# A graph's edges counted in BF16, with a bound in place of a look at the counts, in a graph network kernel on one Trainium2 core

## The chip, the core and the metric

The kernel runs on one core of a Trainium2 chip. A core has a matrix engine (PE; its weight loads are shown as PEld), a vector engine (DVE), a scalar engine (ACT), a general engine (POOL), a queue for transfers (SP) and DMA engines that move data between the chip's memory and the core. Each engine works through its own list of instructions in order; semaphores tie the lists together. The metric is the time of one execution on the device, in microseconds; lower is better.

## The reference

A graph network over N = 3125 nodes with D = 256 features. There are two edge lists: list a, 100000 edges (src, dst) sorted by dst, and list b, 65536 edges of a graph attention layer (GAT). Cut to what matters here:

```python
xn = layernorm(x)
x = x + gnn0(xn) + mix(xn)          # convolution over list a; 4 layers of linear attention and feed-forward
x = x + ffn0(layernorm(x))          # GAT over list b gates four experts
xn = layernorm(x)
x = x + gnn1(xn) + attention1(xn)   # two aggregations over list a; linear attention
x = x + ffn1(layernorm(x))          # eight experts, the two best for each row

def gnn0(x):
    agg = segment_sum(x[src], dst, num_segments=N)
    return batchnorm((x + agg) @ W.T + b)

# in GAT, with a loop added for every node
e = leaky_relu(a_src[src] + a_dst[dst], negative_slope=0.2)
ee = exp(e - segment_max(e, dst)[dst])
alpha = ee / (segment_sum(ee, dst)[dst] + 1e-16)
agg = segment_sum(h[src] * alpha, dst)
```

Every segment sum over a list is computed as a product with a matrix of counts: entry (s, d) says how often the edge from s to d is in the list.

## The kernel before

**Counting.** The matrix AT (FP32, 3125 x 3125, in the chip's memory) holds the counts of list a, C those of list b. Both are first cleared by 25 transfers of 1528 KB each (`clear`, L454). Then each list is taken in columns of 128 edges; a's has 782 columns, b's 512. `Edges.prepare` (L311) finds for every edge how many equal ones come before it in a window of columns: one DVE comparison a column (L343, in `prepare_tail` L383) with its output in a scratch tile `junk`, whose sum goes to `val`, and five small operations a chunk (L353 to L357) that make the addresses. `scatter` (L390) then adds `val` to the matrix with one indirect transfer a column, issued by POOL (L394). Scatters of one window are free of each other; a window waits for the window before.

**The order of the edge work.** The generator `both` (L413) writes it out: eight chunks of list a are prepared before the mix starts, then chunks of a alone, then pairs of a window of a (5 or 4 columns) with two columns of b; last comes the rest of b, 198 columns in windows of 16. The mix calls `beside` after each of its steps, which moves the generator on by 1.05 steps. Scatters of both lists stand on POOL in that order. Between two barriers (`tc.no_sync_barrier`) a list scheduler of the framework may exchange instructions on an engine; POOL's order of the lists is held by explicit dependencies.

**The mix.** Four layers, each with a QKV part (L564 to L578), a softmax part (to L617) and an output and feed-forward part whose results are added to xs on DVE (L639, L652).

**The convolution.** After the barrier at L695, `aggregate` (L657) reads AT row block by row block (`ch`, L673), takes the greatest count of each block on DVE (L675, into `most`), and multiplies the FP32 rows of `xn` with it (L680); L688 adds the node itself with an identity. `done0` (L709) copies the sums to aT, multiplies with the weights and collects batch norm's statistics.

**GAT.** The front (L821) normalises xs and makes the attention terms; the first pass (L872 on) reads C as `cnt` (L880), turns it into penalties on ACT (L884) and takes maxima on DVE (L887, output in a scratch tile `am` with one buffer). The second pass (L917 on) weighs and sums. In it `copy_counts` has POOL copy AT to A1, the same counts in BF16, in 25 pieces (L933), and `most` becomes `more`, which says whether a count is over 256, so that BF16 doesn't hold it exactly.

**Layer 1.** `sums` (L1406) multiplies three BF16 parts of each row (`parts`) with A1 (L1430). A branch (`if_more`, L1595 and L1651) adds what A1 lost; with these inputs `more` is 0 and the branch is passed over.

Of the kernel before, what the change touches and what calls it, by code (L numbers as in the profile page):

```python
# [17 lines left out]
P = 128  # L18
# [27 lines left out]
COLS = 32  # L46
CLR = 3056
# [37 lines left out]
def tile_gps(ctx: ExitStack, tc: tile.TileContext, a, out):  # L85
# [207 lines left out]
    class Edges:  # L293
# [7 lines left out]
        def __init__(self, ep, w_before, dump, key, width, used, rows, mat, tag):  # L301
            self.ep, self.w_before, self.dump = ep, w_before, dump
            self.key, self.used, self.rows = key, used, rows
            self.flat = mat.rearrange("(n o) -> n o", o=1)
            self.val = ep.tile([P, width], F32, name=f"val{tag}", tag=f"val{tag}")
            self.idx = key[:, :].bitcast(I32)
            self.before, self.started, self.queued = [], [], []
            self.width, self.made, self.have = width, 0, (0, 0)
            self.ps = None

        def prepare(self, cols, win):  # L311
# [7 lines left out]
            for c in range(c0, c1, win):  # L319
# [20 lines left out]
                for j in range(k):  # L340
                    junk = ep.tile([P, WIDE * P], BF16, name="junk", tag="junk", bufs=2)
# [12 lines left out]
            V.scalar_tensor_tensor(sel[:, :w], val, BEFORE, sel[:, :w], op0=OP.is_lt, op1=OP.mult)  # L354
            V.tensor_tensor(rel[:, :w], kc, dump[:, :w], op=OP.subtract)
# [4 lines left out]
        def prepare_tail(self, c, k):  # L360
# [9 lines left out]
            for j in range(k):  # L370
                for i, (h, w) in enumerate(halves):
                    junk = ep.tile([P, WIDE * P], BF16, name="junk", tag="junk", bufs=2)
# [17 lines left out]
        def scatter(self, c, end, other=None):  # L390

            if c < self.used:
# [3 lines left out]
                    in_=self.val[:, c:c + 1], in_offset=None, compute_op=OP.add)  # L396
# [16 lines left out]
    def both(ea, eb, clear_b):  # L413
# [27 lines left out]
        while eb.made < eb.width:  # L441
            c0 = eb.made
            yield from eb.prepare(COLS, TAIL)
            for c in range(c0, eb.made):
                eb.scatter(c, (c - c0) % TAIL == TAIL - 1 or c == eb.made - 1)
# [4 lines left out]
    with ExitStack() as st:  # L450
# [3 lines left out]
        def clear(mat):  # L454

            m = mat.rearrange("(p b f) -> p b f", p=P, f=CLR // 4)
            for b in range(25):
                nc.sync.dma_start(m[:, 4 * b:4 * b + 4, :], zero[:, None, :].to_broadcast([P, 4, CLR // 4]))
                yield
# [10 lines left out]
        first, later = clear(AT), clear_own()  # L470
# [5 lines left out]
        steps(first, 4)  # L476
        with tc.tile_pool(name="ps_keys", bufs=1, space=PSUM) as ps:
            key_a = keys(ep, ps, a["src"], a["dst"], E0, True, "a")
            steps(first, 3)
# [35 lines left out]
        ea = Edges(ep, w_before, dumpf, *key_a, AT, "a")  # L515
        behind = both(ea, Edges(ep, w_before, dumpf, *key_b, C2, "b"), later)
# [140 lines left out]
    def aggregate(ps, ap, X, nfb, self_id, passes, done, most, shared):  # L657


        for groups in passes:  # L660
            c0, c1 = 512 * groups[0], min(N, 512 * (groups[-1] + 1))
            bank, acc = None, {}
            for i, g in enumerate(groups):
                if g == shared:
                    bank = ps.tile([P, nfb, P], F32, name="agb", tag="agb", bufs=1)
                for fb in range(nfb):
                    acc[fb, i] = (bank[:, fb, :] if g == shared else
                                  ps.tile([P, 512], F32, name=f"ag{fb}_{i}", tag=f"ag{fb}_{i}", bufs=1))
            for s in range(NT):
                r = rows_of(s)  # L670
                ch = ap.tile([P, 512 * 3 + cols_of(NG - 1)], F32, name="ch", tag="ch", bufs=3)
                for q0, q1 in split_rows(r):
                    nc.sync.dma_start(ch[q0:q1, :c1 - c0], AT2[s * P + q0:s * P + q1, c0:c1])  # L673
                at = passes.index(groups) * NT + s
                V.tensor_reduce(most[:r, at:at + 1], ch[:r, :c1 - c0], axis=AX.X, op=OP.max)  # L675
                for fb in range(nfb):
                    w = X[:r, s, fb * P:(fb + 1) * P]
                    for i, g in enumerate(groups):
                        n = cols_of(g)
                        T.matmul(acc[fb, i][:, :n], lhsT=w, rhs=ch[:r, i * 512:i * 512 + n],  # L680
                                 start=s == 0 and (g != shared or fb == 0),
                                 stop=s == NT - 1 and (g != shared or fb == nfb - 1), skip_group_check=g == shared)
                if s == 0:
                    for fb in range(nfb):
                        for i, g in enumerate(groups):
                            for j, t in enumerate(tiles_of(g)):
                                q = rows_of(t)
                                T.matmul(acc[fb, i][:, j * P:j * P + q], lhsT=X[:q, t, fb * P:(fb + 1) * P],  # L688
                                         rhs=self_id[:q, :q], start=False, stop=False, skip_group_check=g == shared)
            for i, g in enumerate(groups):  # L690
                for fb in range(nfb):
                    done(i, g, fb, acc[fb, i], cols_of(g))
# [3 lines left out]
    most_p = ctile([P, 1], "most_p")  # L696
    more = ctile([1, 1], "more", I32)
    with ExitStack() as st:
        gp = st.enter_context(tc.tile_pool(name="gnn0", bufs=1))
        xn = gp.tile([P, NT, D], F32, name="xn", tag="xn")  # L700
        for g in range(NG):
            load_rows(xn[:, 4 * g:4 * g + len(tiles_of(g)), :], xn_d, g)
# [4 lines left out]
        stats = gp.tile([P, 2, NG, 6], F32, name="stats", tag="stats")  # L707
        with tc.tile_pool(name="ps_g0", bufs=1, space=PSUM) as ps:
            def done0(i, g, fb, p, n):  # L709
                if fb:  # L710
                    S.activation(aT[:, fb, 512 * g:512 * g + n], p[:, :n], AF.Copy)
# [8 lines left out]
                else:  # L720
                    V.tensor_copy(aT[:, fb, 512 * g:512 * g + n], p[:, :n])

            most = gp.tile([P, 2 * NT], F32, name="most", tag="most")
            V.memset(most, 0.0)
            aggregate(ps, gp, xn, 2, ident, [[0, 1, 2], [3, 4, 5, 6]], done0, most, NG - 1)
            V.tensor_reduce(most_p, most, axis=AX.X, op=OP.max)
# [54 lines left out]
    with ExitStack() as st:  # L781
# [135 lines left out]
        with ExitStack() as st2:  # L917
# [5 lines left out]
            p = ptile()  # L923
            T.transpose(p[:1, :P], most_p, ident)
            V.tensor_reduce(most_p[0:1, :], p[0:1, :P], axis=AX.X, op=OP.max)
            V.tensor_scalar(more, most_p[0:1, :], MOST, None, op0=OP.is_gt)
            copies = iter(range(25))

            def copy_counts(after):

                b = next(copies, None) if after else None
                if b is not None:
                    d = G.dma_start(out=A1.rearrange("(p f) -> p f", p=P)[:, CLR * b:CLR * (b + 1)],  # L933
                                    in_=AT.rearrange("(p f) -> p f", p=P)[:, CLR * b:CLR * (b + 1)])
                    tc.add_manual_dep(d.ins, after.ins.name, Edges.after, reason="beside the second pass")

# [77 lines left out]
            def summed(g, s, ex, c, m, state):  # L1014
# [6 lines left out]
                for h in range(4):  # L1021
                    at = 20 * s + 5 * h
                    o = T.matmul(pa[32 * h:32 * h + 32, c:c + m], lhsT=hgp[:r, at:at + 32], rhs=ex[:r, h, c:c + m],  # L1023
                                 start=(s == 0), stop=(s == NT - 1))
                if c + m < n:
                    return
                if s % 3 == 2:
                    copy_counts(state.get("gone"))
                    state["gone"] = o
# [365 lines left out]


    def parts(pool, x, xb):

        r, w = x.shape
        rest = pool.tile([P, w], F32, name="rest", tag="rest", bufs=3)[:r]  # L1400
        S.activation(xb[:, 0, :], x, AF.Copy)
        G.tensor_tensor(rest, x, xb[:, 0, :], op=OP.subtract)
        S.activation(xb[:, 1, :], rest, AF.Copy)
        G.tensor_tensor(xb[:, 2, :], rest, xb[:, 1, :], op=OP.subtract)

    def sums(ps, ap, Xb, nfb, passes, done, shared=None):  # L1406


        for groups in passes:
            c0, c1 = 512 * groups[0], min(N, 512 * (groups[-1] + 1))  # L1410
            bank = None
            acc = {}
            for i, g in enumerate(groups):
                if g == shared:
# [383 lines left out]
```

## Time and profile before

| | us |
|---|---|
| median of 3 runs | 5104.12 |
| the three runs | 5093.92, 5104.12, 5104.90 |
| the profiled execution, whole | 5094.23 |
| its span | 5092.4 |
| PE busy in the span | 4003.0 |
| DVE busy | 3218.2 |
| POOL busy | 2769.6 |
| ACT busy | 1467.1 |

The profile records one execution; its span is the time from its first to its last record, and 1.8 us of the execution lie around it. The granted clock of PE was 0.865 of full speed over the span. A line of a group names the kernel's line, engine, operation, output and input, then count, busy time, mean duration in ns, and the idle time of the engine in front of these instructions with what ended it. A line of a timeline has the start in us from the span's start, the duration, the instruction, and in brackets the idle time before it with its releaser. The stages in the trace: the mix with the edge work from the start to about 2257, the convolution and GAT's front to 2682, GAT's first pass to 3057, its second to about 3690, then layer 1.

### The profile page before, as it was taken

How to read it: one execution, taken by the hardware profiler on the slowest of the kernel's cores; microseconds unless marked ns; L12 is line 12 of the kernel's file. 1: busy time of each engine (PE TensorE's matmuls, PEld its weight loads, DVE VectorE, ACT ScalarE, POOL GpSimd, SP SyncE). 2: the span in 40 equal slices, each digit the busy share in tenths (PEclk: the TensorE clock that was granted, in tenths of full speed). 3: DMA queues.
4: the chain of work that ended last, by engine and by line, in shares of the span. 5: the costliest groups of instructions: out<-in, count | busy, mean ns of one | idle time of the engine just before them, and what ended most of it. 6: DMA issues, size and time to landing. Idle time of an engine off the chain costs nothing. (4 is left out here: it accounts for less than half of the span.)

```text
span 5092.4 us, 48980 instructions
## 1 busy us (share of the span) xinstructions
PE 4003.0 (79%) x16189; PEld 2300.3 (45%) x16189; DVE 3218.2 (63%) x8074; ACT 1467.1 (29%) x2293; POOL 2769.6 (54%) x1860
## 2 busy tenths in 40 slices
PE   1457888878766877849979964666689998999999
PEld 1234455445544454524446641222245444544477
DVE  7978887898899874113348996889973031331231
ACT  0311133114111321200014448989740021000033
POOL 0668888888888888877760006888620031001034
PEclk6668888889787878969989986888899999999999
DMA  9954444444332322247656536543291212212266
GB/s 371 329 117 74 83 72 55 81 79 56 26 26 17 34 16 1 5 88 138 131 101 216 186 123 176 138 121 104 84 280 55 83 50 70 64 54 68 57 170 169
DMA packets 457112, 530.76 MB, mean 104 GB/s; under 512 B 213682, under 2 KB 354779, under 8 KB 451798
## 3 DMA queue, kind: packets, MB, share of 16 engines
q1 hardware_dynamic: 256058, 494.24, 30.7%
q0 software_dynamic: 200784, 33.23, 13.9%
q8 instruction: 133, 2.18, 0.2%
q14 instruction: 137, 1.11, 0.1%
HBM read 397.41 MB, written 169.95 MB: 111 GB/s over the span
## 5 line engine op out<-in xcount | busy, mean ns | idle before, releaser
L394 POOL DMA_INDIRECT AT<-vala,keya x782 | 1232.6, 1576 | 421.0 <-issue 221.0
L394 POOL DMA_INDIRECT C<-valb,keyb x512 | 807.6, 1577 | 203.4 <-issue 143.0
L988 POOL TENSOR_TENSOR ex<-ex,pqb 128x1024 f32<-128x1024 f32 (+3 forms) x200 | 367.0, 1857 | 434.0 <-ACT ex L987 433.4
L343 DVE SCALAR_TENSOR_TENSOR junk<-kr,keya,w_before 128x640 bf16<-128x640 f32 (+2 forms) x729 | 573.1, 830 | 0.6 <-DMA kr<-keys_a 0.6
L383 DVE SCALAR_TENSOR_TENSOR junk<-kr,keyb,w_before 128x1024 bf16<-128x1024 f32 (+1 forms) x390 | 482.3, 1269 | 4.5 <-DMA kr<-keys_b 4.4
L194 PE MATMUL tr<-ident,rows 128*128 128x128 f32 (+1 forms) x500 | 103.4, 361 | 465.8 <-ACT rows L180 441.0
L228 PE MATMUL mm<-hT,w 128*128 128x512 f32 (+1 forms) x896 | 418.2, 632 | 17.2 <-ACT hT L196 16.9
L1430 PE MATMUL ag<-chb,Hb 128*128 128x512 bf16 (+1 forms) x1800 | 420.1, 387 | 13.0 <-DMA chb<-A 13.0
L887 DVE CUSTOM_DVE_ANT_0 am<-asb,pen 128x1664 f32<-128x1664 f32 (+3 forms) x200 | 357.3, 1786 | 51.0 <-ACT pen L884 41.0
L649 PE MATMUL o<-w,hid 128*128 128x256 f32 (+1 forms) x1600 | 383.0, 393 | 0.0
L1023 PE MATMUL pa<-ex,hgp 128*32 128x512 f32 (+3 forms) x1400 | 208.4, 676 | 197.1 <-DVE ex L1011 193.9
L1011 DVE SCALAR_TENSOR_TENSOR ex<-ex,ct 128x2048 f32<-128x2048 f32 (+3 forms) x175 | 345.7, 2007 | 23.4 <-ACT ex L1004 13.8
L1004 ACT ACTIVATE ex<-ex,as 128x1024 f32<-128x1024 f32 (+3 forms) x400 | 345.2, 932 | 3.4 <-DVE ex L993 2.9
L649 PEld LDWEIGHTS o<-w,hid 128*128 128x128 f32 (+1 forms) x1600 | 296.9, 190 | 79.4 <-issue 34.7
L1259 POOL DMA_INDIRECT slots<-rb,r_ati x50 | 49.8, 997 | 516.2 <-DVE rb L1252 407.6
L680 PE MATMUL ag<-ch,xn 128*128 128x512 f32 (+1 forms) x600 | 272.5, 602 | 62.3 <-issue 62.3
L231 ACT ACTIVATE hid<-mm,fm 128x512 f32<-128x512 f32 (+1 forms) x336 | 211.1, 632 | 370.4 <-PE mm L228 353.0
L228 PEld LDWEIGHTS mm<-hT,w 128*128 128x128 f32 x896 | 191.7, 233 | 234.9 <-issue 190.0
L194 PEld LDWEIGHTS tr<-ident,rows 128*128 128x128 f32 (+1 forms) x500 | 66.7, 174 | 506.6 <-ACT rows L180 469.2
L180 ACT ACTIVATE rows<-xs,ln_nmr,rs_y 128x256 f32<-128x256 f32 (+1 forms) x200 | 105.7, 592 | 649.0 <-DVE ln_nmr L173 625.1
L1430 PEld LDWEIGHTS <-Hb 128*128 128x128 bf16 (+1 forms) x2100 | 184.9, 99 | 226.9 <-issue 35.1
L675 DVE TENSOR_REDUCE most<-ch 128x1 f32<-128x1536 f32 (+3 forms) x50 | 89.0, 1780 | 228.7 <-DMA ch<-AT 228.5
(430 smaller groups left out, 6962.5 us busy)
## 6 DMA issues: line engine op xcount, KB each, us to landing
AT<-zero SPq DMA_DIRECT2D x25, 1528.0 KB
C<-zero SPq DMA_DIRECT2D x25, 1528.0 KB
cnt<-C SPq DMA_DIRECT2D x24, 1562.5 KB
cd<-C SPq DMA_DIRECT2D x36, 1024.0 KB
kr<-keys_b SPq DMA_DIRECT2D x64, 512.0 KB
f1w<-in_f_w_dram SPq DMA_DIRECT2D x56, 512.0 KB
slots<-blank SPq DMA_DIRECT2D x15, 1820.0 KB
kr<-keys_a SPq DMA_DIRECT2D x48, 512.0 KB
```

The lines of the kernel that those rows point to most:

```text
L228: T.matmul(ph[:, :n], lhsT=w1[:, k, hb * P:(hb + 1) * P], rhs=xT[:, k, :n], start=(k == 0), stop=(k == 1))
L231: S.activation(h[:, :n], ph[:, :n], AF.Gelu, bias=bias[hb])
L343: V.scalar_tensor_tensor(junk[:, :k * P], self.kr[:, at:at + k * P], key[:, c + j:c + j + 1], self.w_before[:, u:u + k * P], op0=OP.is_equ ...
L383: V.scalar_tensor_tensor(out, kk, key[:, c + j:c + j + 1], by, op0=OP.is_equal, op1=OP.mult, accum_out=more[:, j:j + 1] if i else self.val ...
L394: s = G.indirect_dma_start(out=self.flat, out_offset=bass.IndirectOffsetOnAxis(ap=self.idx[:, c:c + 1], axis=0), in_=self.val[:, c:c + 1], ...
L649: T.matmul(po[:r], lhsT=hid[hb][:, j * P:j * P + r], rhs=w2[:, hb, :], start=(hb == 0), stop=False)
L680: T.matmul(acc[fb, i][:, :n], lhsT=w, rhs=ch[:r, i * 512:i * 512 + n], start=s == 0 and (g != shared or fb == 0), stop=s == NT - 1 and (g ...
L887: V.tensor_tensor_reduce(out=junk[:r, :w], in0=asb[:r, h, c0:c1], in1=pen[:r, :w], scale=1.0, scalar=-3.0e38, op0=OP.subtract, op1=OP.max, ...
L988: G.tensor_tensor(e, e, pq[:r, h, :n], op=OP.add)
L1004: S.activation(ex[:r, h, :n], ex[:r, h, :n], AF.Exp, bias=sc)
L1011: V.scalar_tensor_tensor(e4, e4, 1.0, ct[:r, None, :m].to_broadcast([r, 4, m]), op0=OP.min, op1=OP.mult)
L1430: T.matmul(acc[fb, g][:, :n], lhsT=Xb[:r, s, i, fb * P:(fb + 1) * P], rhs=ch[:r, at:at + n], start=first, stop=last, skip_group_check=g == ...
```

## The change

List a is counted straight into A1 in BF16; AT is neither cleared nor filled unless a branch asks for it. While a list with a BF16 matrix is prepared, each chunk also notes, for either half of the targets, the greatest count that a window adds at one place (`most`); the sum of these over the windows is a bound on every count in that half. `at_most` forms the two sums after the mix, and `more` says whether the larger is over 256. If it is, `recount` clears AT, scatters all of list a again in FP32, copies AT to A1, and `residue` adds what A1 lost. The convolution uses `sums` with three BF16 parts of the rows, made in front of the branch, and an identity in BF16 for the node itself. The 198 last columns of b are prepared as before, but their scatters stand behind the branch. The scratch tile `junk` has one buffer instead of two. GAT's second pass has no copies any more.

```diff
@@ class Edges, __init__
+            self.low = None
+            if mat.dtype == BF16:
+                self.low = ep.tile([P, width], BF16, name=f"low{tag}", tag=f"low{tag}")
+                self.most, self.windows = ep.tile([P, 2, MOSTW], BF16, name=f"most{tag}", tag=f"most{tag}"), 0
+                V.memset(self.most, 0.0)
@@ prepare, and the same in prepare_tail
-                    junk = ep.tile([P, WIDE * P], BF16, name="junk", tag="junk", bufs=2)
+                    junk = ep.tile([P, WIDE * P], BF16, name="junk", tag="junk", bufs=1)
@@ prepare, between L354 and L355
+            if self.low is not None:
+                S.activation(self.low[:, c0:c1], val, AF.Copy)
+                n = w // win
+                i, self.windows = self.windows, self.windows + n
+                part = small.tile([P, COLS], F32, name="e_part", tag="e_part", bufs=1)
+                V.tensor_scalar(part[:, :w], kc, 1.0 / N, 8388608.0, op0=OP.mult, op1=OP.add)
+                V.tensor_scalar(part[:, :w], part[:, :w], -8388608.0, None, op0=OP.add)
+                V.scalar_tensor_tensor(part[:, :w], kc, 1.0 / N, part[:, :w], op0=OP.mult, op1=OP.is_ge)
+                V.tensor_tensor(rel[:, :w], sel[:, :w], val, op=OP.mult)
+                V.tensor_tensor(part[:, :w], part[:, :w], rel[:, :w], op=OP.mult)
+                for j in range(2):
+                    if j:
+                        V.tensor_tensor(part[:, :w], rel[:, :w], part[:, :w], op=OP.subtract)
+                    V.tensor_reduce(self.most[:, j, i:i + n], part[:, :w].rearrange("p (n w) -> p n w", w=win),
+                                    axis=AX.X, op=OP.max)
@@ scatter
-                    in_=self.val[:, c:c + 1], in_offset=None, compute_op=OP.add)
+                    in_=(self.val if self.low is None else self.low)[:, c:c + 1], in_offset=None, compute_op=OP.add)
@@ new in Edges
+        def at_most(self, ps):
+            top = small.tile([P, 2, 2], F32, name="e_top", tag="e_top")
+            V.memset(top, 0.0)
+            q = ps.tile([P, P], F32, name="mq", tag="mq", bufs=1)
+            for j in range(2):
+                for i in range(2):
+                    n = min(P, MOSTW - i * P)
+                    p = ps.tile([P, P], BF16, name="mt", tag="mt", bufs=2)
+                    T.transpose(p[:n], self.most[:, j, i * P:i * P + n], ident_b)
+                    V.tensor_reduce(top[:n, i, j:j + 1], p[:n], axis=AX.X, op=OP.max)
+            for i in range(2):
+                T.matmul(q[:1, :2], lhsT=ones_col, rhs=top[:, i, :], start=(i == 0), stop=(i == 1))
+            return q[:1, :2]
+        def recount(self, zero, mat, low):
+            f = CLR // 4
+            m = mat.rearrange("(p b f) -> p b f", p=P, f=f)
+            for b in range(25):
+                nc.sync.dma_start(m[:, 4 * b:4 * b + 4, :], zero[:, None, :].to_broadcast([P, 4, f]))
+            for c in range(self.used):
+                G.indirect_dma_start(
...
+            for b in range(25):
+                G.dma_start(
...
@@ both, the rest of b
-                eb.scatter(c, (c - c0) % TAIL == TAIL - 1 or c == eb.made - 1)
+                tail.append((c, (c - c0) % TAIL == TAIL - 1 or c == eb.made - 1))
@@ clear, and what is cleared and counted into
+            z = zero if mat.dtype == F32 else zero.bitcast(BF16)
+            n = 4 if mat.dtype == F32 else 5
-        first, later = clear(AT), clear_own()
+        first, later = clear(A1), clear_own()
-        steps(first, 4)
+        steps(first, 2)
-            steps(first, 3)
+            steps(first, 2)
-        ea = Edges(ep, w_before, dumpf, *key_a, AT, "a")
+        ea = Edges(ep, w_before, dumpf, *key_a, A1, "a")
@@ aggregate is removed; parts, sums, residue and if_more move up; in sums
+                for g in groups if own is not None and s == 0 else []:
+                    for fb in range(nfb):
+                        for j, t in enumerate(tiles_of(g)):
+                            q = rows_of(t)
+                            for i in range(3):
+                                T.matmul(acc[fb, g][:, j * P:j * P + q], lhsT=Xb[:q, t, i, fb * P:(fb + 1) * P],
+                                         rhs=own[:q, :q], start=False, stop=False, skip_group_check=g == shared)
@@ layer 0's convolution
+        S.activation(aT, ones_col[:, 0:1, None].to_broadcast([P, 2, N]), AF.Copy, scale=0.0)
+        S.activation(less, ident, AF.Copy, scale=-1.0)
+            V.tensor_reduce(most, ea.at_most(ps), axis=AX.X, op=OP.max)
+            V.tensor_scalar(more, most, MOST, None, op0=OP.is_gt)
+            for t in range(NT):
+                r = rows_of(t)
+                if t % 4 == 0:
+                    xg = work.tile([P, 4, D], F32, name="xg", tag="rows")
+                    load_rows(xg, xn_d, t // 4)
+                x = xg[:r, t % 4, :]
+                S.activation(xb[:r, t, 0, :], x, AF.Copy)
+                for i in range(2):
+                    p = ps.tile([P, D], F32, name="rest", tag="rest", bufs=5)
+                    T.matmul(p[:r], lhsT=ident[:r, :r], rhs=x, start=True, stop=False)
+                    for k in range(i + 1):
+                        T.matmul(p[:r], lhsT=less[:r, :r], rhs=xb[:r, t, k, :], start=False, stop=(k == i))
+                    S.activation(xb[:r, t, i + 1, :], p[:r], AF.Copy)
+        with (
...
+              if_more()):
...
+            ea.recount(zero, AT, A1)
+            residue(ps, rp, xb, 2, add0)
+        for c, end in tail:
+            eb.scatter(c, end)
...
-            aggregate(ps, gp, xn, 2, ident, [[0, 1, 2], [3, 4, 5, 6]], done0, most, NG - 1)
-            V.tensor_reduce(most_p, most, axis=AX.X, op=OP.max)
+            sums(ps, gp, xb, 2, [[0, 1, 2], [3, 4, 5, 6]], done0, shared=NG - 1, own=ident_b)
@@ GAT's second pass
-            copies = iter(range(25))
-            def copy_counts(after):
...
-                    copy_counts(state.get("gone"))
```

## The prediction

> **What bounds the kernel now.** I read the page first (busy shares, costliest groups), then POOL's timeline around the end of the mix, the waits of PE and DVE there, the busy time by stage, and last DVE's timeline instruction by instruction. The span is 5092.4 us and no engine fills it, so it has to be read by stage. Three stages touch the change: the mix with the edge work beside it (0 to 2257), the convolution with the rest of list b (2257 to 2682), and the GAT passes.
>
> ```profile
> L394 POOL DMA_INDIRECT AT<-vala,keya x782 | 1232.6, 1576 | 421.0 <-issue 221.0
> L394 POOL DMA_INDIRECT C<-valb,keyb x512 | 807.6, 1577 | 203.4 <-issue 143.0
> ```
>
> Each scatter holds POOL 1.55 us and the next follows 0.30 later: 1.86 apart, 1294 x 1.86 = 2407 us in one unbroken order. POOL's timeline (start, us; idle before and its releaser in brackets), PE's waits (us in total, times, longest) and the timelines of PE and ACT show what this order releases:
>
> ```profile
> 2247.45 1.55 POOL L394 DMA_INDIRECT AT<-vala,keya  x1 [1.97 <-DMA AT<-vala,keya]
> ...
> 2257.26 1.55 POOL L394 DMA_INDIRECT C<-valb,keyb  x1 [4.54 <-DMA C<-valb,keyb]
> ...
> 2667.21 1.55 POOL L394 DMA_INDIRECT C<-valb,keyb  x1 [5.57 <-DMA C<-valb,keyb]
> ```
>
> ```profile
> PE ag L680 <- issue: 62.3, 1, 62.3
> ```
>
> ```profile
> 2197.22 0.63 PE L220 MATMUL o<-rows,ones_row 1*53 1x256 f32 x2
> 2260.12 7.91 PE L680 MATMUL ag<-ch,xn 128*128 128x512 f32 x12 [62.27 <-issue]
> ```
>
> ```profile
> 2682.38 3.09 ACT L884 ACTIVATE pen<-cnt,big 128x1664 f32<-128x1664 f32 x2 [1.59 <-DMA cnt<-C]
> ```
>
> The mix ends at 2198; PE then idles 62 us for the last AT scatter. The convolution runs 2260 to 2555, its batch norm and the GAT front to about 2661. But GAT's first pass starts when cnt arrives, and cnt waits for the last C scatter (2667). So **the end of list b's tail sets the rest of the program**; the convolution chain has 10 to 20 us to spare. Stage by stage (PE, PEld, DVE, ACT, POOL busy, then clock, DMA share, GB/s):
>
> ```profile
> 368.00:700.00 332.00, 252.58 (x841) 150.51 (x840) 296.69 (x1063) 58.41 (x90) 275.82 (x179) 0.85 0.48 80
> 842.00:1170.00 328.00, 255.84 (x844) 152.13 (x845) 291.66 (x1049) 58.41 (x90) 274.05 (x178) 0.85 0.49 79
> 1319.00:1700.00 381.00, 261.02 (x863) 155.76 (x864) 353.29 (x731) 58.64 (x91) 318.09 (x205) 0.80 0.30 23
> 1846.00:2198.00 352.00, 281.39 (x920) 168.37 (x920) 134.46 (x355) 62.34 (x102) 294.39 (x190) 0.83 0.25 5
> ```
>
> The FFN stages of mix layers 0 to 2 are nearly full on DVE because of the key comparisons; layer 3 has DVE to spare.
>
> **The change, part by part.**
>
> *POOL's start.* A's BF16 matrix is half the bytes: 39.1 MB become 19.6, and the stage 60:80 moves 393 GB/s, so 50 us less clearing. The first scatter (113.9 now) comes at about 64; the chunks it needs are ready by then, and the chain, whose 1.86 pitch is POOL's own, ends at 2197 instead of 2247. BF16 values change nothing in the pitch; the new copy to `low` on ACT (33 of some 0.3 us) lies beside. The clears were also in front of the key loads on SP: 2 + 2 of 1.96 MB instead of 4 + 3 of 1.53, so DVE starts about 5 us earlier. x (K, issued 96.7) and C's clears behind it come up to 40 us sooner on SP as well; worth nothing, since DVE is busy with the held chunks until 114.7 before it turns to x.
>
> *The tail behind the branch.* The 198 scatters of b now stand on POOL behind `more`, which needs the end of the mix on PE and DVE. Behind that wait stand only these scatters; cnt, and with it GAT, waits for them. Price of the step: four transposes and reduces, two matmuls, a reduce and a compare, about 4 us; loading the register about 4 (DVE's old L1595: branch at 4083.5, semaphore 4086.6); the jump. The row of the old branch is 0.05 us on POOL and 3.83 on PE. POOL's old body was empty, PE's had thousands of matmuls; the new POOL body has 807 DMAs. [...] I take PE's row, 4 us, not POOL's. Sum 12 (bounds 5 and 25). The tail begins at the later of 2197 and mix end + 12. **The mix end, no longer POOL, sets the tail.**
>
> *`junk` with one buffer.* Each of some 1,490 comparisons now writes the tile the one before wrote. With two buffers:
>
> ```profile
> 109.23 1.30 DVE L343 SCALAR_TENSOR_TENSOR junk<-krp,keya,kr_w 128x1024 bf16<-128x1024 f32 x1
> 110.44 1.30 DVE L343 SCALAR_TENSOR_TENSOR junk<-krp,keya,kr_w 128x1024 bf16<-128x1024 f32 x1
> ...
> 2743.48 1.89 DVE L887 CUSTOM_DVE_ANT_0 am<-asb,pen 128x1664 f32<-128x1664 f32 x1
> ...
> 2745.29 0.17 DVE L901 TENSOR_TENSOR z<-z,att_dst 128x16 f32<-128x16 f32 x1
> 2745.41 1.89 DVE L887 CUSTOM_DVE_ANT_0 am<-asb,pen 128x1664 f32<-128x1664 f32 x1
> ```
>
> A comparison of 1.30 us is followed after 1.21: the next starts 0.09 before the end. `am` has one buffer already: the L887 before ends at 2745.37, an independent small operation starts 0.08 before that end, but the next L887 0.04 after it. So a shared tile costs 0.12 us a pair. [...] The trace shows 0.12, so I follow the row: at most 1,490 x 0.12 = 179 us of DVE, at least nothing. Small operations between two comparisons fit into the hold, which takes off some 20 and hides most of the new bound operations (33 chunks x 8 = 264, which would be 22 us at 0.085 alone).
>
> What of it reaches the mix end? Pairs with no mix operation between, times 0.12, less what idle DVE takes up: held chunks +7, the earlier start -5, first QKV +4. In the FFN stages I let 60% of DVE's idle time, waits for PE of about 1 us each, take it up. Layer 0 (368 to 731): 398 comparisons, +36 against 41 idle, leaves 11. Layer 1: 391, +35 against 22 (19 more lie in one wait, L617 for PE, that moves along), leaves 22. Layer 2: 259, +25 against 14, leaves 17. The later QKV stages, where mix operations lie between the comparisons, 2 together; layer 3 nothing. Sum 58: the mix ends at 2256 and the tail begins at 2268, **+11** against 2257.
>
> *The tail itself.* Its 15 waits for C sum to 47.9 us; with half the matrix loads beside them I take **-8** (bounds 0 and -20).
>
> *The convolution.* 25 x (2 + 3) small matmuls and three ACT copies for xb, with aT's clearing, come before it: 25 x 2.3 = 58 us if each tile's chain is waited out, 31 if PE runs on; take 55, partly beside the wait for the branch. The sums are those of the second convolution (L1430: 3884.2 to 4082.8, 199 us) plus 150 identity matmuls, 15: 214 instead of 295. So it ends at 2256 + 55 + 214 = 2525, 30 before today; its front, 106 us, is over at 2631, some 50 before cnt's turn at 2268 + 404 + 13 = 2685. The 81 us saved are **0** on the path; if the tail were gone they would count down to that margin. The 50 max reduces (89 us of DVE) lay beside PE: 0. xg's seven loads take the place of xn's on SP.
>
> *GAT's second pass.* 25 copies leave POOL: 13.4 us and 34.5 idle in front of them, bounds 0 and -48. The pass has POOL at 78%, DVE at 86, ACT at 88, none full, and copies end 170 us before it does; nearest is the POOL time itself, **-18**.
>
> Sum: +11 - 8 - 18 = -15. Against the profiled execution (5094.2) 5079; against the median of 5104.12, which two of three runs support, 5089. I say 5085. About 10 us (0.2%) is what a measurement here can tell from nothing.
>
> **The rivals.**
>
> *The hold isn't taken up* (25 in 100). If DVE's extra lies ahead of PE's operands, the mix slips 90 to 140 instead of 58. For it: DVE is at 89 to 93% in three FFN stages. Against: PE alone needs 352 in layer 3, so PE has room. At 115 the tail begins at 2325, +68; -26 gives +42: 5136 to 5146. It decides from a slip of 73 (break-even) and shows as slower from 83.
>
> *No hold at all* (20). If the same-tile write needs no wait, the mix slips about 5, the tail begins at 2215: -42 - 26 = -68, 5026 to 5036. [...] Against: L887.
>
> *The convolution sets the end* (5). Only if xb takes over 100 us; then up to 30 later than my sum.
>
> *The recount runs* (1). From the reference's lists, the sum over windows of the greatest count is 156 for one half of the targets and 173 for the other; the limit is 256. If taken: 782 x 1.86 = 1455 us more.
>
> **How the numbers follow.** My forecast has 49 in 100, its own range 5060 to 5105: faster 0.32, same 0.13, slower 0.04. Unabsorbed hold: 0.02 same, 0.23 slower. No hold: faster 0.20. The last two: 0.01 same, 0.05 slower. Together 0.52, 0.16, 0.32. The range 5030 to 5145 holds all but the ends of the two rivals.
>
> **What would show it.** First scatter near 64; comparisons 0.04 after the end of the last one, not 0.08 before; mix end near 2256; POOL idle from about 2197 until 12 us after it; convolution near 215 us and PE waiting before GAT; cnt released by C's tail near 2672. If the mix ends before 2215 or after 2290, the absorption or the hold is wrong; if GAT starts without waiting for C, the path is.

## The result, and the profile after

The kernel before took 5102.58 us (median of 10 runs, 5085.20 to 5108.35), the changed one 5068.23 (10 runs, 5057.26 to 5085.88). The ratio is 0.994, with a 95% interval of 0.9926 to 0.9955: some 31 us, or 0.6%, less. The changed kernel's profiled execution has a span of 5064.4 us, 28.0 under that of before.

The stages of the two profiled executions, and of a second one of the changed kernel (the run `after_again` below). "GAT starts" is the first `pen`, in us from the span's start:

| | before | after | after again |
|---|---|---|---|
| first scatter of list a | 113.9 | 65.9 | 65.3 |
| last scatter of list a | 2247.4 | 2178.2 | 2173.9 |
| mix ends (last xs) | 2198.0 | 2249.8 | 2240.0 |
| tail of list b starts | 2257.3 | 2197.7 | 2191.2 |
| convolution's sums start | 2260.1 | 2324.7 | 2315.9 |
| last scatter of list b | 2667.2 | 2611.9 | 2602.0 |
| GAT starts | 2682.4 | 2669.8 | 2661.1 |
| first pass ends | 3054.0 | 3041.4 | 3032.7 |
| layer 1's sums start | 3884.2 | 3864.6 | 3851.8 |
| from there to the end | 1208.2 | 1199.8 | 1199.7 |

So the 28.0 us of the profile are 12.6 until GAT starts, 7.0 in GAT's second pass, and 8.4 in the rest. The rest has the same code in both; over all kernels below it takes 1195.7 to 1210.6, and the kernels with GAT's copies (1195.7, 1202.6 and 1208.2) lie on both sides of the changed kernel's 1199.8, so its share is not read as an effect of the change.

The first readings are the two scatter lists. First the group lines of the changed kernel's page, then POOL's timeline at the ends of the lists (the same columns as before):

```profile
L418 POOL DMA_INDIRECT A<-lowa,keya x782 | 1224.7, 1566 | 369.4 <-issue 219.0
L418 POOL DMA_INDIRECT C<-valb,keyb x512 | 794.2, 1551 | 220.9 <-issue 136.7
```

```profile
65.91 1.68 POOL L418 DMA_INDIRECT A<-lowa,keya  x1 [61.74 <-DVE e_part L376]
...
2178.17 1.54 POOL L418 DMA_INDIRECT A<-lowa,keya  x1 [2.64 <-DMA A<-lowa,keya]
...
2197.68 1.54 POOL L418 DMA_INDIRECT C<-valb,keyb  x1 [14.28 <-DMA C<-valb,keyb]
...
2611.87 1.54 POOL L418 DMA_INDIRECT C<-valb,keyb  x1 [2.51 <-DMA C<-valb,keyb]
```

POOL never waits for the mix. The tail starts at 2197.68, after a wait of 14 us for the scatters of the window before, while the mix runs on to 2250. The source puts all 198 scatters of the tail behind the branch; in the program, 59 of them stand in front of it (the trace has 59 between the tail's start and POOL's last step at the branch). The list scheduler moved them there: between its barriers nothing bound them to the source's order. What that does is seen at the branch (line 823 is `if_more()`). First come the queues' instructions there: under `PEldq` and `POOLq` the trace has the branch and semaphore instructions of PE and POOL, and the three numbers are min/median/max in ns, then first and last start. Then come SP's first loads of A1 for the convolution, and PE's first product:

```profile
L823 PEldq COMPARE_BRANCH  x1: 4967/4967/4967, 2291.1 to 2291.1; - x1
L823 POOLq COMPARE_BRANCH  x1: 53/53/53, 2304.6 to 2304.6; - x1
L823 POOLq INC_SWDGE_SEM  x1: 1567/1567/1567, 2319.8 to 2319.8; - x1
L823 POOLq EVENT_SEMAPHORE  x4: 17/43/7934, 2307.9 to 2319.7; - x4
```

```profile
2321.57 4.40 SPq L743 DMA_DIRECT2D chb<-A  x8
```

```profile
2324.68 5.34 PE L750 MATMUL ag<-chb,xb 128*128 128x512 bf16 x18 [33.40 <-DMA chb<-A]
```

PE is past its own branch at 2296. POOL comes to its own at 2304.6, when 52 of its 59 scatters have begun; the last of the other seven starts at 2315.7. POOL waits 7.9 us on one semaphore and is done at 2319.8 + 1.57 = 2321.4. The convolution's loads of A1 are issued 0.2 us after that, and PE waits 33.4 us for them. The branch's body contains POOL transfers that write A1, which the author takes for the reason why the loads stay behind POOL's passing of the branch; that they do stay behind it is tested below, the reason was not shown. The other end of the stage, on ACT:

```profile
2669.23 0.69 ACT L232 ACTIVATE hid<-mm,fm 128x512 f32<-128x512 f32 x1 [17.39 <-PE mm L229]
2669.81 3.08 ACT L1002 ACTIVATE pen<-cnt,big 128x1664 f32<-128x1664 f32 x2
```

`pen` follows `hid`, an expert's layer that stands in front of it on ACT, with no wait for cnt. `hid` waits for PE, and PE for rows that go through memory (PE's timeline):

```profile
2665.80 6.83 PE L229 MATMUL mm<-xfg,f0w 128*128 128x512 f32 x12 [14.38 <-DMA xfg<-xf_d]
```

These rows come at the end of the convolution and of the GAT front. **So this chain now sets when GAT starts**, and not list b's tail, whose last scatter started 58 us earlier. The loads of cnt didn't follow that scatter at once: SP issues them in its order behind the front's transfers, at 2654.4.

```profile
2652.27 1.48 SPq L985 DMA_DIRECT2D asb<-as_d  x2
2653.80 0.57 SPq L925 DMA_DIRECT2D xfg<-xf_d  x1
2654.41 1.18 SPq L998 DMA_DIRECT2D cnt<-C  x2
```

The same `hid` stood there before the change (ACT's timeline of the kernel before):

```profile
2680.11 0.69 ACT L231 ACTIVATE hid<-mm,fm 128x512 f32<-128x512 f32 x1 [18.70 <-PE mm L228]
```

It ended at 2680.8, and `pen`, after 1.6 us more for cnt, began at 2682.4. The two chains had been almost level.

The hold of the shared tile is on DVE as forecast. A comparison of the first feed-forward stage ends at 401.47, and the next starts at 401.51:

```profile
400.72 0.75 DVE L350 SCALAR_TENSOR_TENSOR junk<-kr,keya,w_before 128x512 bf16<-128x512 f32 x1
401.51 0.75 DVE L350 SCALAR_TENSOR_TENSOR junk<-kr,keya,w_before 128x512 bf16<-128x512 f32 x1
```

### The profile page after: what moved, and what is told of

The parts are those of the page before. It is cut to its first block, busy times and chain, and to the rows that moved or that the text cites. A ratio compares the mean times of both kernels' runs of the same rounds, so it can differ in the third digit from the quotient of the medians.

```text
span 5064.4 us, 50451 instructions
## 1 busy us (share of the span) xinstructions
PE 4018.7 (79%) x16771; PEld 2309.4 (46%) x16771; DVE 3209.6 (63%) x8299; ACT 1499.4 (30%) x2396; POOL 2734.7 (54%) x1835
## 5 line engine op out<-in xcount | busy, mean ns | idle before, releaser
L418 POOL DMA_INDIRECT A<-lowa,keya x782 | 1224.7, 1566 | 369.4 <-issue 219.0
L418 POOL DMA_INDIRECT C<-valb,keyb x512 | 794.2, 1551 | 220.9 <-issue 136.7
L350 DVE SCALAR_TENSOR_TENSOR junk<-kr,keya,w_before 128x640 bf16<-128x640 f32 (+2 forms) x729 | 603.4, 828 | 14.7 <-DMA kr<-keys_a 3.3
L407 DVE SCALAR_TENSOR_TENSOR junk<-kr,keyb,w_before 128x1024 bf16<-128x1024 f32 (+1 forms) x390 | 496.2, 1272 | 17.0 <-DMA kr<-keys_b 11.0
L750 PE MATMUL ag<-chb,xb 128*128 128x512 bf16 (+2 forms) x1950 | 399.6, 364 | 34.5 <-DMA chb<-A 34.0
L750 PEld LDWEIGHTS <-xb 128*128 128x128 bf16 (+1 forms) x2100 | 182.9, 97 | 252.1 <-issue 41.8
```

The source lines that it names most:

```text
L350: V.scalar_tensor_tensor(junk[:, :k * P], self.kr[:, at:at + k * P], key[:, c + j:c + j + 1], self.w_before[:, u:u + k * P], op0=OP.is_equ ...
L407: V.scalar_tensor_tensor(out, kk, key[:, c + j:c + j + 1], by, op0=OP.is_equal, op1=OP.mult, accum_out=more[:, j:j + 1] if i else self.val ...
L418: s = G.indirect_dma_start(out=self.flat, out_offset=bass.IndirectOffsetOnAxis(ap=self.idx[:, c:c + 1], axis=0), in_=(self.val if self.low ...
L750: T.matmul(acc[fb, g][:, :n], lhsT=Xb[:r, s, i, fb * P:(fb + 1) * P], rhs=ch[:r, at:at + n], start=first, stop=last, skip_group_check=g == ...
```

## The experiments

Each run is compared with the kernel before on the same chip. They ran in three sets of four, in the order told, except that `best`, told last, ran in the second set; within a set the chip is the same, from set to set it is not.

**The changed kernel again.** No edit; it gives the changed kernel's values beside the next three.

> The changed kernel itself once more, as the measure for the runs beside it. Expected: ratio 0.994 to before; mix end near 2250, first A scatter near 66, the tail of C begun near 2198, the convolution's sums begun near 2325, GAT's first pass near 2670 from the span's start.

Ratio 0.9957 (0.9941 to 0.9973), 5063.6 us. All stages stand as in the first profile, up to 13 us earlier. Differences of some 10 us between single profiles are therefore not read as effects below, unless something else supports them. The mix end varies more: in the seven profiles of kernels that have the changed kernel's mix as it is, it lies between 2228.7 and 2249.8, at 2237 in the mean.

**The tail held behind the branch**, as the prediction had it:

```diff
+        tc.no_sync_barrier()
         for c, end in tail:
             eb.scatter(c, end)
```

> The changed kernel with a barrier between the branch and the 198 scatters of list b's tail, so that the scheduler can't put any of them on POOL ahead of the branch (in the changed kernel 59 stand there). Theory P, the prediction's step (the tail waits for the mix end and sets GAT): POOL idles from about 2185 to the branch, the tail begins near 2262, ends near 2678, GAT's first pass starts near 2693, so +20 to +25 us over the changed kernel, ratio 0.998 to 1.000; the convolution begins earlier, near 2300, without use. Theory Q (only the convolution chain matters, the tail has room): the convolution begins 25 us earlier and the time falls by about 25, ratio 0.989.

Ratio 0.9943 (0.9924 to 0.9962). POOL's timeline, then PE's and ACT's:

```profile
2236.48 1.54 POOL L418 DMA_INDIRECT C<-valb,keyb  x1 [57.73 <-DMA C<-valb,keyb]
```

```profile
2273.62 0.59 PE L750 MATMUL ag<-chb,xb 128*128 128x512 bf16 x1 [6.38 <-PEq L823]
```

```profile
2662.98 3.09 ACT L1003 ACTIVATE pen<-cnt,big 128x1664 f32<-128x1664 f32 x2 [39.49 <-DMA cnt<-C]
```

This is the order that the prediction worked with. The mix ends at 2228.7, POOL idles until 7.8 us after it, the convolution starts 42 us earlier than in the repeat, and all of that is lost again: `pen` waits 39.5 us for the tail, and GAT starts at 2663.0, as in the repeat (2661.1). The two orders happen to be worth the same, one bound by the convolution and one by the tail: that is chance.

**No branch.** The whole `if_more()` block (`recount`, `residue`) is taken out of layer 0; with these inputs it is passed over anyway.

```diff
-        with (tc.tile_pool(name="g0t", ...) as rp, ..., if_more()):
-            ...
-            ea.recount(zero, AT, A1)
-            residue(ps, rp, xb, 2, add0)
```

> The changed kernel without the branch and all that stands in it (the recount and what it adds; not run with these inputs anyway). Theory R (the convolution's loads of A wait until POOL has passed the branch, behind 59 scatters): the convolution begins as soon as xb is there, near 2290 instead of 2325, GAT's first pass near 2635 to 2640, -30 us, ratio 0.988. Theory S (a branch that is passed over costs only its few us on PE): -8 us or less, ratio 0.992 to 0.994.

Ratio 0.9855 (0.9832 to 0.9878): 1.0% of the time, some 49 us against the repeat, is the price of a branch that isn't taken. By both intervals that is uncertain by about 14 us, and only 38 of it are seen in the profiles before GAT.

```profile
2276.78 0.58 PE L750 MATMUL ag<-chb,xb 128*128 128x512 bf16 x1 [0.47 <-ACT xb L821]
```

```profile
2623.31 3.08 ACT L995 ACTIVATE pen<-cnt,big 128x1664 f32<-128x1664 f32 x2
```

The convolution starts as soon as xb is there, 39 us before the repeat's, and GAT starts 38 before the repeat's. The convolution still sets GAT's start (list b's last scatter is at 2594.7).

**A second scratch tile.** From the seventh paired chunk on, `junk` alternates between its own tile and the room of `zero`, which the clears no longer need; `recount` would make its zeros anew.

```diff
-                    junk = ep.tile([P, WIDE * P], BF16, name="junk", tag="junk", bufs=1)
+                    junk = self.scratch()     # alternates between tags "junk" and "zj" (zero's room)
```

> The changed kernel with two scratch tiles for the comparisons again: from the seventh chunk with pairs on, every second comparison writes into the room of the zeros, which are no longer needed by then (the branch would make them anew). The mix should end 35 to 50 us sooner, near 2205, if the hold of 0.12 us a comparison is what moved it. Theory R: the convolution still begins near 2320, since POOL's branch stands behind 59 scatters, so the time is the changed kernel's within 5 us, ratio 0.993 to 0.995. Theory M (the mix end sets the convolution's start): -35 to -50 us, ratio 0.984 to 0.987.

Ratio 0.9952 (0.9935 to 0.9969), the same as the repeat's. DVE's last addition to xs, POOL's branch, and PE:

```profile
2214.20 0.41 DVE L721 TENSOR_TENSOR xs<-xs,o 53x256 f32<-53x256 f32 x1 [16.05 <-PE o L221]
```

```profile
L834 POOLq COMPARE_BRANCH  x1: 53/53/53, 2292.8 to 2292.8; - x1
```

```profile
2313.14 0.58 PE L761 MATMUL ag<-chb,xb 128*128 128x512 bf16 x1 [59.63 <-DMA chb<-A]
```

The mix ends 26 us earlier, and nothing follows: PE waits 59.6 us for A1 instead of 33.4, because POOL comes to the branch at 2292.8 (2295.9 in the repeat).

**The bound taken early.** `at_most` and `more` are formed at the start of the mix's last layer, when all of list a is prepared, and the tail is held behind the branch.

```diff
+            if l == LAYERS - 1:
+                most = small.tile([1, 1], F32, name="most", tag="most")
+                V.tensor_reduce(most, ea.at_most(ps), axis=AX.X, op=OP.max)
+                V.tensor_scalar(more, most, MOST, None, op0=OP.is_gt)
...
+        tc.no_sync_barrier()
         for c, end in tail:
```

> The changed kernel with the bound's two sums formed at the start of the mix's last layer (so that the answer is there before POOL asks for it) and a barrier between the branch and list b's tail (so that POOL's branch comes first, the 198 scatters after). Theory R (the convolution's loads wait for POOL's passing of the branch): POOL passes near 2180, the tail begins near 2195 and ends near 2600, the convolution begins near 2275 to 2285, GAT's first pass near 2625 instead of 2661, ratio 0.986 to 0.989. Rival: the two together gain nothing, as pin_tail alone did not, because the price is in the branch itself: ratio 0.993 to 0.996.

Ratio 0.9886 (0.9869 to 0.9903), 0.7% under the repeat's. POOL is at the branch at 2178.4, right after list a; the tail starts at 2197.8 as in the changed kernel, and PE starts the convolution at 2287.1, 29 us before the repeat's. GAT starts at 2631.8, 29 before too. The branch stays; what stood before it is gone. The early bound without the barrier was not run.

**The hold alone, in the kernel before.**

```diff
-                    junk = ep.tile([P, WIDE * P], BF16, name="junk", tag="junk", bufs=2)
+                    junk = ep.tile([P, WIDE * P], BF16, name="junk", tag="junk", bufs=1)
```

> The kernel before with one scratch tile for the comparisons instead of two, nothing else. If the hold moves the mix end as in the changed kernel, it ends near 2235 to 2250 instead of 2198, still ahead of the last scatter into AT (2247), which the convolution waits for: no change of time, ratio 0.998 to 1.002. Rival: the hold isn't covered here, +40 us, ratio 1.006 to 1.009.

Ratio 1.0002 (0.9992 to 1.0012). Two groups of DVE from the mix's last feed-forward stage, of the kernel before and then of this one (1846 us to the end of the mix):

```profile
L383 DVE SCALAR_TENSOR_TENSOR junk<-kr,keyb,w_before 128x1024 bf16<-128x1024 f32 (+1 forms) x69 | 84.7, 1252 | 1.3 <-DMA kr<-keys_b 1.3
```

```profile
L383 DVE SCALAR_TENSOR_TENSOR junk<-kr,keyb,w_before 128x1024 bf16<-128x1024 f32 (+1 forms) x144 | 182.4, 1267 | 4.0 <-DMA kr<-keys_b 1.7
```

The mix ends at 2207.1 instead of 2198.0: 9 us, no more than two profiles of one kernel differ by. The held comparisons don't push the mix; 75 more of them are carried over into the last stage, where DVE was idle most of the time (busy 134.5 of 352 us in the kernel before). There the last scatter of list a, at 2245.5, covers the 9 us.

**The copies put back.** POOL copies A1 to AT in 25 pieces, at the places in GAT's second pass where the kernel before made its copies; nothing reads them.

```diff
+                    d = G.dma_start(out=AT...[:, CLR * b:CLR * (b + 1)], in_=A1...[:, CLR * b:CLR * (b + 1)])
```

> The changed kernel with 25 copies put back on POOL in GAT's second pass at the old places (from A1 to AT, whose contents nobody reads with these inputs). The prediction's step: +18 us, ratio 0.998 to 0.9995. From the two traces (the pass shorter by about 7 in the changed kernel): +7 us, ratio 0.996 to 0.998. If they cost nothing: 0.994 to 0.996.

Ratio 1.0003 (0.9995 to 1.0011): with the copies, the change is worth nothing. The group of the copies, and the scatters of list a (min/median/max ns, first and last start) here and in the changed kernel:

```profile
L1047 POOL DMA_DIRECT2D AT<-A x25 | 13.4, 535 | 21.7 <-PE pa L1137 20.9 <-issue 0.7 <-PE ct L1123 0.2
```

```profile
L418 POOL DMA_INDIRECT A<-lowa,keya x782: 1552/1554/7439, 65.7 to 2185.7; - x196
```

```profile
L418 POOL DMA_INDIRECT A<-lowa,keya x782: 1542/1543/7117, 65.9 to 2178.2; - x196
```

The second pass takes 839.9 us, against 823.2 and 819.1 without the copies. Also, the scatters take 11 ns more each in the median, from the first one on, long before a copy is issued: list a ends at 2185.7, and between 2172.1 and 2179.5 in the eleven profiles without the copies. GAT starts at 2674.2, against 2661.1 in the repeat and 2669.8 in the first profile. These copies go the other way than those of the kernel before (BF16 to FP32).

**The bound taken out, and the bound and the hold.** In the first kernel the eight operations that each chunk does for the bound are removed, so that `more` is formed from zeros; the second has the second scratch tile as well.

```diff
-                part = small.tile([P, COLS], F32, name="e_part", ...)
-                ... (eight operations)
```

> The changed kernel without the 264 small operations of the bound (the sums are then 0 and the branch is passed over as before). If they lie in the holds, as the prediction had it, the mix ends within 5 us of the changed kernel's 2240 to 2250; if they cost their 0.085 us each, near 2220 to 2228. Either way POOL's branch sets the convolution, so the time stays: ratio 0.993 to 0.996.

> no_bound with two scratch tiles as in two_scratch. What is left of the mix end's shift is then neither the bound nor the hold from the seventh paired chunk on: near 2200 if these two are all of it, near 2215 if most of the rest is the order of work at the start. Time as in no_bound, ratio 0.992 to 0.996, since POOL's branch still stands behind 59 scatters.

Ratios 0.9942 (0.9924 to 0.9959) and 0.9951 (0.9932 to 0.9969): nothing gained by either. The end of the mix in each (DVE's timeline):

```profile
2216.28 0.41 DVE L698 TENSOR_TENSOR xs<-xs,o 53x256 f32<-53x256 f32 x1 [17.09 <-PE o L221]
```

```profile
2199.50 0.41 DVE L709 TENSOR_TENSOR xs<-xs,o 53x256 f32<-53x256 f32 x1 [16.06 <-PE o L221]
```

From the repeat's 2240.0, the bound's removal alone takes 24 us, the second tile alone 26, the two together 40.5; from the mean of seven, 2237, it is 20, 22 and 37. They overlap, and together they are the whole slip: without both, the mix ends where it did before the change (2198.0). The bound's 264 operations at the 0.085 us that the prediction had for one would be 22 us (in the changed kernel the one at 1374.11 is followed 0.08 later by the next operation). The convolution starts at 2314.1 and 2320.7, still behind POOL.

**Two tiles for `am`**, the scratch tile of GAT's first pass:

```diff
-                            junk = ap.tile([P, MID], F32, name="am", tag="am", bufs=1)
+                            junk = ap.tile([P, MID], F32, name="am", tag="am", bufs=2)
```

> The changed kernel with two buffers instead of one for the scratch tile of GAT's first pass (am). DVE fills this pass, so the hold of 0.12 us on each of 200 operations should be on the path: -20 to -25 us, the pass 346 to 352 us long instead of 370, ratio 0.989 to 0.991. If the hold were free [...], nothing: 0.994 to 0.996.

Ratio 0.9891 (0.9872 to 0.991). From DVE's timeline:

```profile
2700.61 1.68 DVE L1005 CUSTOM_DVE_ANT_0 am<-asb,pen 128x1461 f32<-128x1461 f32 x1
2702.21 1.68 DVE L1005 CUSTOM_DVE_ANT_0 am<-asb,pen 128x1461 f32<-128x1461 f32 x1
```

The second starts 0.08 us before the first ends, where one tile made it start 0.04 after. The pass takes 345.1 us instead of 371.6: 26.5 for 200 operations, 0.13 each, and the median falls by 29, against the repeat on another chip. Here the hold is on the path, and its price is the row's, not nothing.

**More of the tail in front of the branch.** 32 more scatters are issued ahead of it, 91 in all:

```diff
-                tail.append((c, (c - c0) % TAIL == TAIL - 1 or c == eb.made - 1))
+                end = (c - c0) % TAIL == TAIL - 1 or c == eb.made - 1
+                if c < 314 + 32:
+                    eb.scatter(c, end)
+                else:
+                    tail.append((c, end))
```

> The changed kernel with 32 more scatters of list b's tail on POOL ahead of the branch (91 instead of 59). Theory R: POOL passes the branch 32 x 1.85 = 59 us and two waits for C, about 66 us, later, the convolution begins near 2382 and GAT's first pass near 2728, +60 to +66 us, ratio 1.006 to 1.009. If the branch on POOL does not hold the convolution: no change, 0.994 to 0.996.

Ratio 1.0058 (1.0039 to 1.0077): slower than before the change. POOL's branch, and PE's first product:

```profile
L827 POOLq COMPARE_BRANCH  x1: 53/53/53, 2362.0 to 2362.0; - x1
```

```profile
2380.40 0.58 PE L754 MATMUL ag<-chb,xb 128*128 128x512 bf16 x1 [106.04 <-DMA chb<-A]
```

32 scatters of 1.85 us are 59; POOL comes to the branch 66 us after the repeat's, the convolution starts 64.5 later and GAT 67. The scatters ahead of the branch set the start of the convolution.

**Early bound, second scratch tile and two tiles for `am` together.**

> early_pin with two scratch tiles for the comparisons (as in two_scratch) and two buffers for GAT's scratch tile am. By theory R the mix end now sets the convolution: mix end near 2205, the convolution begins near 2250; list b's tail, ending near 2600, sets GAT's first pass at 2612 to 2620. With two buffers am's 200 operations lose 0.12 us each, 24 us of a pass that DVE fills: 346 to 352 instead of 370. Together about -70 us to the changed kernel, ratio 0.980 to 0.984. If the hold is no price on a full DVE either, the pass stays at 370 and the ratio is 0.986.

Ratio 0.9802 (0.9783 to 0.9822), 4992.53 us: faster than both kernels. On ACT:

```profile
2616.26 3.09 ACT L1015 ACTIVATE pen<-cnt,big 128x1664 f32<-128x1664 f32 x2 [7.86 <-DMA cnt<-C]
```

The convolution starts at 2259.6, and GAT, at 2616.3, waits 7.9 us for list b: now both chains end nearly together, and the earlier mix end counts, as it didn't in `two_scratch`.

Over all of these, one relation holds: from the convolution's first product to GAT's start it is 344.6 to 349.2 us in the ten profiles in which `pen` waits for no cnt. GAT starts at the later of that and of list b's end. In the kernel before, whose sums were 74 us longer, `hid` ended 420.7 us after the first product. Six of the ten, and `pin_tail`, where cnt sets the start:

| run | convolution starts | GAT starts | difference |
|---|---|---|---|
| no_branch | 2276.8 | 2623.3 | 346.5 |
| early_pin | 2287.1 | 2631.8 | 344.7 |
| two_scratch | 2313.1 | 2657.7 | 344.6 |
| after_again | 2315.9 | 2661.1 | 345.2 |
| copies_back | 2326.6 | 2674.2 | 347.6 |
| more_ahead | 2380.4 | 2728.5 | 348.1 |
| pin_tail (cnt sets) | 2273.6 | 2663.0 | 389.4 |

## Why the prediction was right or wrong

The side was right and the total inside the range (5085 said, 5068 measured; of a gain that the sum had at 15 us, some 31 came), but the path was not: the prediction's own sign of a wrong path, GAT starting without a wait for C, is what the profile shows. That the total came out near is in good part luck: errors of both signs, told below, cancelled.

| step | predicted | measured |
|---|---|---|
| first scatter | 64 | 65.9 |
| list a ends | 2197 | 2178.2 |
| hold of a shared tile | 0.12 us | 0.04 after instead of 0.08 before |
| mix ends | 2256 | 2249.8, 2240.0 (seven profiles: 2228.7 to 2249.8) |
| tail starts | 2268 | 2197.7 |
| convolution's sums | 214 | 220 |
| GAT starts against before | +3 | -12.6 |
| second pass | -18 | -7.0, -11.1 |
| rest | 0 | -8.4, no effect of the change |

- **The step that failed: "The tail begins at the later of 2197 and mix end + 12", with "Behind that wait stand only these scatters".** The source's order was taken for the order on POOL. The scheduler put 59 scatters ahead of the branch, so list b ended 55 us before its old time instead of some 3 after, and the branch came late on POOL instead. `pin_tail` restored the assumed order: then the tail starts 7.8 us after the mix and cnt sets GAT, as said. With that order the step's form was right, its 12 us somewhat high.
- **"The 81 us saved are 0 on the path", with some 50 us to spare.** Two terms of it failed. The first is the margin: "10 to 20 us to spare" before, from a front of 106 us. The front's own work is over at 2661, but ACT has `hid` ahead of `pen`, and with its wait the front is 126 us, and 125 after the change; the margin before was 1.6 us. The second follows from the wrong order: list b's last scatter came 58 us before `pen`, so it no longer held cnt. (SP's order held the load of cnt until 2654.4. In the kernel before, `pen` came 7.2 us after that load's issue, so as an estimate `pen` could have started at 2661.6; the other 8 us it stood behind `hid`.) By the prediction's own start of the sums, 2311, the chain would have been through at 2311 + 345 = 2656; it started at 2324.7 and was through at 2669.8. Against before it started 64.6 us later, with sums 74 us shorter, so the shorter sums did count: they paid for the late start. The rival "the convolution sets the end" was given 5 in 100 and held to be possible only if xb took over 100 us; xb was ready about 2291, and what was late was POOL.
- **The price of the branch, 12 us.** It was charged to the tail alone, and at PE's row, which for POOL was the author's estimate. PE's row was as expected (3.8 to 6.4 us over the runs), and POOL's pass with no scatter in flight took 4 us too (`pin_tail`, 2231.8 to 2235.6); what these times are spent on, no run shows. With scatters in flight POOL's pass took 17 us from its compare to its last semaphore, and A1's loads waited for it, a wait that the prediction hadn't. `no_branch` puts the whole at 38 us before GAT and about 50 in the time.
- **The hold and the bound in the mix.** The sum was too high, and its split wrong. The slip, said to be 58, was 52 and 42, and 39 in the mean of seven profiles (31 to 52). All of it was put on the hold, with the bound's operations hidden in it; the bound's removal takes 20 to 24 of it, the second tile 22 to 26. In `before_junk1` the hold without the bound moved the mix end by 9 alone. The share that DVE's idle time takes up was estimated stage by stage; the comparisons that move on to layer 3 were left out of it. The hold itself is real: `am_two` puts it at 0.13 us for each of 200 operations that share one output tile, so following the row was right, though in the changed kernel's mix it wasn't on the path.
- **List a's end.** 48 us of earlier start were seen; 21 more came off the chain. The scatters' own time, 1.543 instead of 1.555 us, is worth 13 for the 1,096 scatters up to there (782 of a and 314 of b); the other 8 weren't traced. The prediction had held the pitch unchanged.
- **The tail, -8.** It took 414 us, with the stop at the branch in it, instead of 410: no gain. Over the runs it varied from 400 (`early_pin`) to 417 (`pin_tail`), so 8 us more or less can't be told here.
- **The copies, -18.** Taken from one pair of profiles the removal gives 17 to 21 us in the pass; the three profiles with copies mean 836 (830.2 to 839.9), the eleven without 825 (819.1 to 828.8), so about 11. To this comes the shorter scatter, some 13 us up to GAT's start between `copies_back` and the repeat (4 against the first profile). Timed, the copies' return is 0.46%, 23 us (1.0003 against 0.9957, uncertain by about 9), which is the whole gain of the change within its intervals. All else that it does adds up to about nothing. The prediction had that too (+3), by other terms, which is luck.
- **The recount** was passed over, as said.

## What to carry to other kernels

Here a branch that wasn't taken held the convolution until the last engine had passed it: PE was past at 2296, POOL at 2321.4, and A1's loads were issued 0.2 us later. With a branch, ask for each engine what stands in front of the branch, and which later loads wait until that engine has passed it, and form its condition as early as its inputs allow. Where a scheduler may exchange instructions, the place of an instruction in the source says nothing on its place in the queue; read it from the program's order before working out who waits. A saving off the path can still pay for a delay that the same change brings, so work out both chains to the point where they meet, and look how near their ends are.

## What the runs showed of the hardware that was not expected

- POOL's pass of an untaken branch whose body has transfers of its own took 17 us with scatters in flight (2304.6 to 2321.4; 14 to 19 over the runs) and 4 us with none (`pin_tail`: 2231.8 to 2235.6). PE's, at the same branch, was 3.8 to 6.4 us in all runs whose rows were read.
- POOL's scatter took 1.554 or 1.555 us in the median in the three kernels with the copies in GAT's second pass, and 1.543 or 1.544 in the others, long before any copy runs. The cause was not settled.
- A scratch tile written by each of two operations in turn cost DVE 0.12 to 0.13 us a pair even though nobody reads it: the second started 0.04 us after the end of the first instead of 0.08 before (the rows of `am` and of the comparisons), and in `am_two` 200 operations were 26.5 us shorter together.
